# First layer of a two-layer scan network: the outer products of a pair of states split over two steps, a masking moved ahead of a product, parts of a softplus one step on

## The chip, the cores and the metric

The kernel runs on one core of a Trainium2 chip, in float32 throughout. The metric is the device time of one execution in microseconds. The core has five engines that each work through a list of their own and wait for each other by semaphores: TensorE (PE; PEld is its loading of weights), VectorE (DVE), ScalarE (ACT), GpSimd (POOL) and SyncE (SP), which here only starts DMA transfers. Matmul results go to PSUM, eight banks of 128 partitions with room for 512 float32 each; everything else is in SBUF or, between the stages, in DRAM.

## What is computed

Two layers of a vision state-space network, one behind the other, on 4 images of 64x64 positions and 192 channels. Each layer normalizes by groups, projects to 384 inner channels and a gate, scans the inner channels along the positions in four directions (by rows, by columns, and both backwards), normalizes the sum, multiplies by the gate and projects back. The change is in the first layer's scan. In the reference:

```python
delta = jax.nn.softplus(delta + delta_bias[None, :, None])
...
def step(h, inp):
    dt, ut, bt, ct = inp
    dA = jnp.exp(dt[..., None] * A_k[None])
    dBu = dt[..., None] * bt[:, :, None, :] * ut[..., None]
    h = dA * h + dBu
    y = jnp.einsum('bkdn,bkn->bkd', h, ct)
    return (h, y)
h0 = jnp.zeros((Bb, K, D, N), u.dtype)
...
_, ys = jax.lax.scan(step, h0, inps)
```

There are K = 4 directions, D = 384 channels, N = 16 states and 4096 positions. The matrix `A` is -n for state n = 1 to 16 (`A_logs` is the logarithm of 1 to 16 for every channel), so the decays of state n are the n-th powers of those of state 1.

## The kernel before

**Rounds and steps.** `FirstLayer.scans` does not walk position by position. It takes blocks of 30 positions (`RW`), the block of each of the four directions at once: 137 rounds (`NR`). Partitions 0 to 63 hold directions 0 and 1 (30 positions each, and four rows for the state carried over from the block before), partitions 64 to 127 directions 2 and 3; the free axis is 4 images x 384 channels = 1536 columns (`W`). A round has 16 steps, one for each state, from n = 16 down to n = 1 (`state(s) = NS - s % NS`); s counts steps through all rounds. So step 0 of a round has state 16, an even state belongs to an even step, and two states, an even step and the odd one behind it, make a pair.

**What one state needs.** Within a block the scan is a matrix product: the output at position l is the sum over the positions l' before it of C(l)·B(l') times the decay from l' to l times dt·u at l'. The decay is put into two factors.

- `outer(s)` (lines 1046 to 1055, TensorE) makes C(l)·B(l') for the two states of the pair (s, s+1) and all four images: two matmuls with a contraction of 8 rows, 128 columns of weights (`at_b`) and 256 columns of data (`cs`) each, into the two halves of one PSUM bank, tile `o`. The pool `pso` has one such tile, so a pair's first matmul waits until the pair before has been read.
- `cut_b(s)` (1057, VectorE) multiplies that bank, 128x512, by a mask that keeps l' up to l and writes `b` to SBUF. The pool has three of them.
- `grown(s)` (1062) makes `x`, dt·u times the n-th power of the growth at l'. For step 0 of a round it is a product of `dtu` with an exponential (line 1068); for each further step the tile of the step before times a factor `f` (line 1072). GpSimd does 1024 of the 1536 columns and VectorE 512, six steps ahead (`AHEAD`); seven tiles. In line 1068 VectorE's factor is the half bank `m[:, 1]` in PSUM (this is called the near product below), GpSimd's is `g` in SBUF.
- `mix(s, j)` (1074, TensorE) is the product itself, b times x, added into the accumulators. j is a half: a half is four 64x64 matmuls (two halves of the rows, two of the columns) with 384 columns of data, one in each quadrant of the array. `accs[0]` and `accs[1]`, two PSUM tiles of two banks, take half 0 and half 1.
- `weigh(s, j)` (1083, VectorE, line 1089) then multiplies accumulator j, 128x768, by the decay `fd`: with the states in falling order this is Horner's rule. In the last step `end_y` (line 962) does it and writes `y`.
- In every odd step ScalarE copies both accumulators to `sx` before they are weighed (`keep_end`, 1028), from which SyncE takes the rows of the carried state (`shrink`), ScalarE and GpSimd decay it (`decay`, `settle`) and SyncE writes it to DRAM (`carry_out`) for the next round (`carry_in`).

**What a round needs ahead of its first step.** `Round.steps` (974) lists this work with an offset in steps from the round's start and an engine; it runs among the steps of the rounds before, at the place `planned(s, engine)`. An offset of -20 is step 12 of a round, and -16 is step 0 of the round just ahead. A softplus of four products makes dt: `v(j)` (TensorE, one product for each half j), `parts(j)` (ScalarE: absolute value to `e`, relu to `up`), `exp(j)` (ScalarE, line 867: `e` becomes exp(-e)), `plus` (ScalarE, 871: `l` = e + 1), `rounded` (GpSimd, 875: `d` = l - 1), `log` (ScalarE, 878: `l` becomes its logarithm) and `delta(j, 0..3)` (TensorE: `up` + `e` - `d` + `l` summed up in PSUM tile `p` by products with a unit matrix). Then come `times_u`, `keep_dt`, sums along the block by a triangle matrix, and their exponentials. The products of this work that have a helper's shape all stand at line 845: eight 64x64 matmuls with 384 columns, or the 26-row form of `v`. Lines 899 and 913 are products of 128x128 with 512 columns. `sums_near` (913), `first_near` (916: the exponential into `m[:, 1]`), `fall_near` (920) and the near product follow each other in steps 9 and 10. The tile `p`, which is `m` in the code, exists once, so each of its uses waits for the readers of the use before. `steps` also lists `sums_d(0)` at -5, -3 and -2, whose results nobody reads.

**The order.** It is written out by hand (`tc.manual_schedule`): the loop over s at line 1094 issues the work of step s, and each engine gets its instructions in that order. TensorE's list of a step is: both halves of `mix(s + 1)`, the planned products, and in an even step `outer(s + 4)`. VectorE's is: both `weigh(s)`, `grown(s + 6)`, in an even step `cut_b(s + 2)`, the planned ones. ScalarE's is: in an odd step both copies, then the planned ones, then in an odd step `decay(s - 2)`. GpSimd's is: `grown(s + 6)`, in an odd step `settle(s - 4)`, the planned ones.

## Time and profile before

| | |
|---|---|
| three runs | 9029.12, 9060.8, 9049.5 us; median 9049.5 |
| the profiled execution | 9056.89 us, its span from first to last instruction 9055.1 |
| granted TensorE clock, mean over the span | 0.95 of full |
| VectorE's near products (L1068), first and last start | 695.5 and 7225.3 us, 137 of them |
| L1078, `mix` on TensorE | 35072 matmuls, mean 502 ns, 3552.2 us busy |
| L1089, `weigh` on VectorE | 4110, mean 958 ns, 195.2 us idle before them, 151.4 of it for TensorE's L1078 |
| L1028, copies on ScalarE | 2192, mean 800 ns, 1072.5 us idle before them, 1032.2 for TensorE's L1078 |
| L1072 on GpSimd | 2055, mean 2368 ns, 323.0 us idle before them |

One float32 matmul of the code is two matmul rows of the profile, so a step's product (both halves, four matmuls each) is a row with x16, the two outer products of a pair are x4 and a helper product is x8. Busy times of TensorE overlap: the end of a matmul is modelled, and the next one starts while it drains. Therefore the text below reads TensorE by the distance between the starts of its rows. In a timeline a bracket at the end of a row gives the engine's idle time just before it and the engine, tile and line that ended it. The stretches of the kernel ahead of the scan (the projections) and behind it (normalization, output, the whole second layer) are not touched.

### The profile page before, as it was taken

To read this page: it belongs to the slowest core of one execution; us is meant where nothing else is said; L and a number is where in the kernel's file an instruction comes from. 1 tells how busy PE (TensorE), PEld (TensorE's weight loads), DVE (VectorE), ACT (ScalarE), POOL (GpSimd) and SP (SyncE) were. 2 spreads that over 40 slices of the span, in tenths; PEclk is the share of its full clock that TensorE was granted. 3 is DMA by queue.
4 is the path that set the end of the run, shared out by engine and by line. 5 is a ranking of instruction groups with operands and counts; after the bars stand their busy time and mean duration, and the time that the engine had idled before them with its cause. 6 is when DMAs were issued, how large, how long until landed. Compare 5 with 4: busy or idle time off the path is not lost. (4 is left out here: it accounts for less than half of the span.)

```text
span 9055.1 us, 193788 instructions
## 1 busy us (share of the span) xinstructions
PE 8209.4 (91%) x64280; PEld 3630.8 (40%) x64280; DVE 7520.8 (83%) x10238; ACT 6193.2 (68%) x10104; POOL 6605.8 (73%) x3814
## 2 busy tenths in 40 slices
PE   8989999999999999999999999999999945786668
PEld 4433333333333333333333333333333335443457
DVE  3328999999999999989999999999999954786766
ACT  3337777777777777777777777777777745575668
POOL 0008999999999999999999999999999932001460
PEclk9999999999999999999999999999999977887789
DMA  6652333333332333333333333333333389343558
GB/s 186 212 183 65 74 76 75 79 74 75 76 78 73 75 78 77 74 77 83 82 84 86 83 83 83 82 83 83 82 83 83 83 211 252 107 138 125 162 140 284
DMA packets 952262, 971.20 MB, mean 107 GB/s; under 512 B 550175, under 2 KB 802732, under 8 KB 950368
## 3 DMA queue, kind: packets, MB, share of 16 engines
q1 hardware_dynamic: 946192, 951.97, 38.7%
q0 software_dynamic: 5056, 6.66, 0.6%
q8 instruction: 520, 8.52, 0.4%
q14 instruction: 494, 4.05, 0.1%
HBM read 521.83 MB, written 375.80 MB: 99 GB/s over the span
## 5 line engine op out<-in xcount | busy, mean ns | idle before, releaser
L1072 POOL TENSOR_TENSOR x<-x,f 128x1024 f32<-128x1024 f32 x2055 | 4865.9, 2368 | 323.0 <-issue 102.9
L1089 DVE TENSOR_TENSOR acc<-acc,fd 128x768 f32<-128x768 f32 x4110 | 3751.4, 958 | 195.2 <-PE acc L1078 151.4
L1078 PE MATMUL acc<-x,b 64*64 64x384 f32 x35072 | 3552.2, 502 | 69.2 <-DVE yt L962 62.6
L1028 ACT COPY sx<-acc 128x768 f32<-128x768 f32 x2192 | 1712.8, 800 | 1072.5 <-PE acc L1078 1032.2
L1078 PEld LDWEIGHTS acc<-x,b 64*64 64x64 f32 x35072 | 1056.2, 132 | 2084.6 <-DVE acc L1089 1397.3
L1072 DVE TENSOR_TENSOR x<-x,f 128x512 f32<-128x512 f32 x2055 | 1387.0, 675 | 0.1
L1052 PE MATMUL o<-cs,at_b 8*128 8x256 f32 x4384 | 1238.0, 401 | 3.7 <-DVE b L1060 3.5
L1052 PEld LDWEIGHTS o<-cs,at_b 8*128 8x128 f32 x4384 | 727.0, 184 | 772.4 <-DVE b L1060 363.1
L837 ACT ACTIVATE cs<-at_c,own 8x256 f32<-8x256 f32 x2192 | 979.8, 494 | 3.5 <-PE o L1052 3.5
L1060 DVE TENSOR_TENSOR b<-o,masks_f 128x512 f32<-128x512 f32 x1096 | 746.7, 681 | 5.7 <-PE o L1052 5.7
L462 PE MATMUL pp<-xT,w_in 96*128 96x512 f32 x1536 | 715.0, 617 | 20.9 <-ACT pad L1286 20.4
L875 POOL TENSOR_SCALAR d<-l 128x1536 f32<-128x1536 f32 x137 | 201.0, 1467 | 671.0 <-ACT l L871 669.9
L845 PE MATMUL p<-dt,steps_f 64*64 64x384 f32 x5480 | 580.0, 493 | 5.0 <-DVE dtu L890 1.9
L1300 DVE SCALAR_TENSOR_TENSOR acc<-pad,conv_w_s,acc 128x2048 f32<-128x2048 f32 x192 | 440.7, 2343 | 48.6 <-ACT acc L1298 47.4
L965 POOL TENSOR_TENSOR yt<-yt,yold 128x1536 f32<-128x1536 f32 x137 | 472.9, 3452 | 0.0
L929 ACT ACTIVATE fd<-p,shift 128x768 f32<-128x768 f32 x274 | 246.7, 900 | 300.2 <-PE p L845 300.2
L462 PEld LDWEIGHTS pp<-xT,w_in 96*128 96x128 f32 x1536 | 292.3, 197 | 370.3 <-issue 341.9
L1041 POOL TENSOR_TENSOR back<-back,small 128x96 f32<-128x96 f32 x1096 | 424.0, 387 | 14.4 <-DMA small<-sx 9.6
L549 PE MATMUL op<-w_out,v 128*128 128x192 f32 x1536 | 289.2, 346 | 136.8 <-DVE ot L552 92.4
L1038 ACT ACTIVATE back<-tot,late_f 128x96 f32<-128x96 f32 x1096 | 409.6, 374 | 0.0
L1281 POOL MEMSET pad<- 128x66 f32 x12 | 1.9, 159 | 553.6 <-DVE acc L1300 386.4
L1068 POOL TENSOR_TENSOR x<-dtu,g 128x1024 f32<-128x1024 f32 x137 | 324.4, 2368 | 80.2 <-ACT g L904 77.6
(218 smaller groups left out, 9542.8 us busy)
## 6 DMA issues: line engine op xcount, KB each, us to landing
x<-carry SPq DMA_DIRECT2D x4384, 24.0 KB
ut<-uT SPq DMA_DIRECT2D x548, 180.0 KB
small<-sx SPq DMA_DIRECT2D x2192, 24.0 KB
carry<-back SPq DMA_DIRECT2D x1096, 48.0 KB
zg<-gate SPq DMA_DIRECT2D x64, 768.0 KB
yold<-y_row SPq DMA_DIRECT2D x546, 90.0 KB
y_row<-yt SPq DMA_DIRECT2D x546, 90.0 KB
y_col<-yt SPq DMA_DIRECT2D x546, 90.0 KB
```

The costliest lines, as they stand in the source:

```text
L462: self.tc.nc.tensor.matmul(pp, self.w_in[:, i, e * 128 : (e + 1) * 128], self.xT[:, i, t * LC : (t + 1) * LC], start=(i == 0), stop=(i == ...
L837: nc.scalar.mul(self.cs[part][:, :, b, :], at_c[self.r % 2][:, at : at + PART, :], own[:, b : b + 1])
L845: nc.tensor.matmul(self.m[half(b), a, :DI], w(a, 2 * b + j), t(a, 2 * b + j), start=start and n == 0, stop=stop and n == len(terms) - 1, s ...
L965: nc.gpsimd.tensor_tensor(self.y, self.y, yold, ALU.add)
L1028: nc.scalar.copy(paired(sxs[s], j), accs[j][:, :, :DI])
L1041: nc.gpsimd.tensor_tensor(back[s], back[s], small[s], ALU.mult)
L1052: nc.tensor.matmul(outs[s][:, at], at_b[p][:, n, :], cs[:, n % PART].rearrange("q b l -> q (b l)"), start=True, stop=True, skip_group_chec ...
L1060: nc.vector.tensor_tensor(bs[s], o, bc(masks, 2, NB), ALU.mult)
L1072: engine.tensor_tensor(xs[s][:, part], xs[s - 1][:, part], f, ALU.mult)
L1078: nc.tensor.matmul(accs[j][half(c), r, :DI], bs[s - s % 2][half(r), s % 2, b, :], xs[s][half(r), cols(b)], start=s % NS == 0, stop=state(s ...
L1089: nc.vector.tensor_tensor(acc, acc, paired(of(s).fd, j), ALU.mult)
L1300: nc.vector.scalar_tensor_tensor(acc, part(tap), weight(tap), acc, ALU.mult, ALU.add)
```

## The change

Three things are changed, all in `FirstLayer.scans`.

1. `outer` takes the half h as an argument and issues one of the two matmuls. Half 0 stays where both were, at the end of an even step s, for the pair s + 4. Half 1 is issued in the next, odd step, between the two halves of that step's `mix`.
2. In the one step of a round in which `grown` on VectorE is the near product (step 10), `cut_b` now comes before it. In all other steps the order stays.
3. `exp(1)` goes from offset -18 to -17, `plus` from -17 to -16, `rounded` from -16 to -15 and `log` from -15 to -14. `exp(0)` and the products `delta` that read the results stay.

```diff
-                        r += [(2 * j - 20, "act", s(self.exp, j))]
+                        r += [(3 * j - 20, "act", s(self.exp, j))]
...
-                    r += [(-17, "act", self.plus), (-16, "pool", self.rounded), (-15, "act", self.log)]
+                    r += [(-16, "act", self.plus), (-15, "pool", self.rounded), (-14, "act", self.log)]
...
-            def outer(s):
-                outs[s] = ps_o.tile([128, LC], F32, name="o")
+            def outer(s, h):
+                if h == 0:
+                    outs[s] = ps_o.tile([128, LC], F32, name="o")
                 cs, p = of(s).cs[s % NS // PART], of(s).r % 2
-                for h in range(2):
-                    n = state(s) - 1 - h
-                    at = slice(h * NB * HALF, (h + 1) * NB * HALF)
-                    nc.tensor.matmul(
-                        outs[s][:, at], at_b[p][:, n, :], cs[:, n % PART].rearrange("q b l -> q (b l)"),
-                        start=True, stop=True, skip_group_check=True,
-                    )
+                n = state(s) - 1 - h
+                at = slice(h * NB * HALF, (h + 1) * NB * HALF)
+                nc.tensor.matmul(
+                    outs[s][:, at], at_b[p][:, n, :], cs[:, n % PART].rearrange("q b l -> q (b l)"),
+                    start=True, stop=True, skip_group_check=True,
+                )
...
-                    if on(s + AHEAD):
+                    if on(s + AHEAD) and (s + AHEAD) % NS > 0:
                         grown(s + AHEAD, nc.vector)
                     if on(s + 2) and s % 2 == 0:
                         cut_b(s + 2)
+                    if on(s + AHEAD) and (s + AHEAD) % NS == 0:
+                        grown(s + AHEAD, nc.vector)
                     planned(s, "dve")
-                    for j in range(2):
-                        if on(s + 1):
-                            mix(s + 1, j)
+                    if on(s + 1):
+                        mix(s + 1, 0)
+                    if on(s + 3) and s % 2 == 1:
+                        outer(s + 3, 1)
+                    if on(s + 1):
+                        mix(s + 1, 1)
                     planned(s, "pe")
                     if on(s + 4) and s % 2 == 0:
-                        outer(s + 4)
+                        outer(s + 4, 0)
```

## The prediction

> **What bounds the kernel now.** I read the page first, then one round of the first layer's scan through, engine by engine. The page says where the time is.

> ```profile
> PE 8209.4 (91%) x64280; PEld 3630.8 (40%) x64280; DVE 7520.8 (83%) x10238; ACT 6193.2 (68%) x10104; POOL 6605.8 (73%) x3814
> ...
> L1052 PE MATMUL o<-cs,at_b 8*128 8x256 f32 x4384 | 1238.0, 401 | 3.7 <-DVE b L1060 3.5
> ```

> The edit touches lines that run in the scan alone, 137 rounds of 16 steps: L1068 on VectorE, once a round, runs from 695.5 to 7225.3 us. The busy time of one round in the windows view (us; busy PE, PEld, DVE, ACT, POOL; clock):

> ```profile
> core 0: us, PE busy (x) PEld busy (x) DVE busy (x) ACT busy (x) POOL busy (x), PEclk, DMA share, GB/s
> 2500.22:2547.87 47.65, 46.15 (x422) 18.00 (x414) 44.55 (x60) 35.46 (x60) 45.20 (x27) 1.00 0.31 76
> ```

> 47.65 us a round. VectorE has 3.1 us to spare in it, GpSimd 2.5, TensorE by this row only 1.5, at the full granted clock. So TensorE comes first, and its rows have to be read by the distance between starts, since a matmul that is shown busy may overlap the next or hide a short wait. Its timeline (start, length, line, operands):

> ```profile
> 2500.58 1.12 PE L899 MATMUL p<-dt,steps_f 128*128 128x512 f32 x2
> 2501.64 1.13 PE L1052 MATMUL o<-cs,at_b 8*128 8x256 f32 x4
> 2502.69 1.52 PE L1078 MATMUL acc<-x,b 64*64 64x384 f32 x16
> 2504.03 0.82 PE L845 MATMUL p<-dt,steps_f 64*64 64x384 f32 x8
> ...
> 2509.89 1.13 PE L913 MATMUL p<-dt,steps_f 128*128 128x512 f32 x2
> 2510.95 1.52 PE L1078 MATMUL acc<-x,b 64*64 64x384 f32 x16
> 2513.24 0.88 PE L845 MATMUL p<-w_dtk_f,xd 26*64 26x384 f32 x8 [0.78 <-DVE x L1068]
> ...
> 2524.12 0.82 PE L845 MATMUL p<-dt,steps_f 64*64 64x384 f32 x8
> 2524.88 1.13 PE L1052 MATMUL o<-cs,at_b 8*128 8x256 f32 x4
> 2526.38 1.74 PE L1078 MATMUL acc<-x,b 64*64 64x384 f32 x16 [0.37 <-DVE yt L962]
> ...
> 2540.62 1.47 PE L1078 MATMUL acc<-x,b 64*64 64x384 f32 x16
> 2541.91 0.82 PE L845 MATMUL p<-d,minus_f 64*64 64x384 f32 x8
> 2542.56 0.82 PE L845 MATMUL p<-l,ident 64*64 64x384 f32 x8
> 2543.31 1.13 PE L1052 MATMUL o<-cs,at_b 8*128 8x256 f32 x4
> ```

> - A step's product with nothing to wait for: 2540.62 to 2541.91, 1.29, so 0.645 a half; a helper product of the same shape also 0.65 (2541.91 to 2542.56).
> - The block of outer products: 2501.64 to 2502.69, 1.055. A half product is two passes of 384 columns in 0.645, 0.84 ns a column; the block is four passes of 256, 0.86. The other 0.195 is its head and tail. L899 streams as many columns (2 x 512) and takes the same 1.06.
> - Entering it: a helper product followed by the block takes 0.75 (2542.56 to 2543.31), 0.11 more than 0.645. Leaving it: the product behind takes 1.34 (2502.69 to 2504.03), 0.05 more than 1.29.

> **What TensorE needs in a round.** 32 half products and 15 helper products at 0.645, three 512-column products and eight blocks at 1.055, 11 entries of 0.11 (six blocks, since two follow L899; three 512-column products; two of 26 rows), nine exits of 0.05: 30.3 + 3.2 + 8.4 + 1.2 + 0.45 = 43.6. The remaining 4.1 is waiting, more than the marked gaps show. 0.84 stands at 2513.24 (from 2510.95 it is 2.29, and the work 0.05 + 1.29 + 0.11 = 1.45), 0.45 at 2526.38 (the second half of the product before began 0.70 ahead of 2524.12, at 2523.42; 2.96 later the next can start, and 0.70 + 0.75 + 1.055 = 2.51 of work lies in that). 2.8 is small waits for VectorE's products with the decay.

> **The split of the outer products.** It takes nothing away and adds, eight times a round, a second head and tail (0.195), a second entry (0.11, now between two half products) and a second exit (0.05): 0.355 a pair, 2.84 a round. TensorE then needs 46.4. What it buys is that the product of an even step starts about 0.43 earlier, since only half a block (0.625) lies ahead of it; VectorE's 0.41 in front of the even steps' L1089 goes. But the second half of that product now stands behind the other half block: taking the round at 2501.64, its first half starts at 2502.26 in place of 2502.69, its second at 2502.26 + 0.70 + 0.11 + 0.625 = 2503.69 in place of 2503.39, 0.3 later, and VectorE waits there instead, at its second L1089. No new semaphore wait comes in: the half that moves reads rows of B and C that are loaded for the round, into a bank that the first half claimed. Queued behind it are the second half product, the planned products and the next half block; VectorE and ScalarE wait for the first.

> Which waits can take up the 2.84? Not the 0.84: L913, ScalarE's L916 and L920, VectorE's L1068 follow each other there, and no half block falls under them (the step's product is an odd one). The 0.45 grows: only 0.70 + 0.75 + 0.625 = 2.07 now lies in the 2.96, so 0.89. Of the small ones I can work out three kinds. Even steps behind one helper product: first half product to its end 0.82, copy 0.80, L1089 0.96, three handovers of 0.06, 2.75 in all, against 1.29 + 0.75 + 0.625 = 2.67 of work: 0.09, at three steps 0.27. The wait for the product with u (mark 0.35, by starts 0.53) loses 0.355 to the added work: 0.18. Behind the round's end, VectorE's chain over one pair is as long as TensorE's work, 4.0 each: 0 to 0.3. That is 0.6; further ones, where VectorE's 44.5 us of work don't fall into place, I can't add up by hand. Ends: 0.3 (nearly all covered) and 1.5 (half of the 2.8 kept). I take 0.9.

> Sum: 46.4 + 0.84 + 0.89 + 0.9 = 49.05, against 47.65: +1.4 a round, 137 rounds +192.

> The unknown in it is the price of a half block *inside* a product, which no row shows. Below, it could be nothing more than streaming (0 instead of 0.355), if loads and drains hide; above, 0.47, if the 0.11 is paid on leaving too. I take 0.355, since rows show every change of shape in both directions at one price.

> [...]

> **Masked B ahead of the near product.** VectorE's timeline:

> ```profile
> 2509.38 1.83 DVE L1089 TENSOR_TENSOR acc<-acc,fd 128x768 f32<-128x768 f32 x2 [0.41 <-PE acc L1078]
> 2512.50 0.69 DVE L1068 TENSOR_TENSOR x<-dtu,p 128x512 f32<-128x512 f32 x1 [1.29 <-issue]
> 2513.10 0.68 DVE L1060 TENSOR_TENSOR b<-o,masks_f 128x512 f32<-128x512 f32 x1
> ```

> L1060 (0.60 from start to start) moves into the 1.29 of idle time; L1068 stays at 2512.50, because it waits for ScalarE's L920, which ends at 2512.41. VectorE is 0.6 earlier behind it, but its next L1089 waits for a ScalarE copy that ends at 2513.14, and the step after for TensorE, whose next product goes through L1068, the helper product and the block. I take 0, ends -0.5 and 0 a round. Were the idle time gone, it would delay L1068 by 0.6.

> **The second exponential, plus, rounding and logarithm one step on.** No instruction is added. ScalarE's queue: L867 (0.73) goes behind two copies that started at 2523.50 after 0.37 idle, so it delayed nothing and now can't; L871 then starts near 2526.9 and ends near 2528.4. GpSimd's L875 falls behind one product of 2.33 and one of 0.35: 2531.45 in place of 2528.77, and TensorE reads it at 2533.42. L878 follows, done by about 2533.7, read at 2535.60; ScalarE's next copies started at 2534.99. 1.9 us of slack each: 0. What covers it is the idle 1.96 and 1.23 in front of ScalarE's copies; without it L878's 1.4 would come on top.

> All is a difference to the profiled execution (9056.89, span 9055.1), 0.08% above the median of 9049.5, so it is added to the median: 9242.

> **Rivals.**
> - *The half block costs only its streaming.* With a price e a pair the round is 43.6 + 8e + 0.84 + 0.89 + 0.9 = 46.2 + 8e. It decides at e = 0.18: below that the kernel is faster; at 0, 46.2, -1.44 x 137 = -197: 8852. For it: 2.8 us of small waits lie in just the places where the half now goes. Against it: the 0.11, 0.195 and 0.05 at every change of shape in the rows. 7%.
> - *The waits swallow the price.* e between 0.16 and 0.20: 9022 to 9077, within 0.3%, about what a measurement of this kernel can tell from no change. Against it: two of the larger waits stay or grow. 5%.
> - *All of it on the path.* 2.84 x 137 = +389: 9438; or the sum above with L878 late by 1.4, 9434. For it: TensorE's 91%. Against it: the waits for VectorE that later products no longer see. 7%.
> - The forecast, a sum with small waits of 0.3 to 1.5 and e of 0.28 to 0.40: 9077 to 9376, 81%.

> Faster 7%, same 5%, slower 88%. The range 9110 to 9365 leaves out the two outer rivals and the forecast's lowest edge.

> **What would show it.** L1052's mean goes from 401 to some 428 ns (its median is 374, so the first of four, with its load in view, takes 482; now it is the first of two); its rows stand alone with 0.62 to the next product, and inside a step's product in every odd step; L1068 on VectorE repeats every 49 us; the idle time of L1089 for TensorE grows from 151 us to over 400; L875 and L878 gain no waiters. A half block under 0.5 us, or a round under 47.65, would prove me wrong; L845's helper products waiting for L875 or L878 would put the loss in the wrong place.

## The result, and the profile after

The changed kernel takes 9492.6 us (median of 4 runs, 9491.47 to 9501.06) against 9052.73 for the one before (9029.12 to 9060.8): a ratio of 1.0492, 95% interval 1.0472 to 1.0513. It is 440 us slower. The forecast was 192 slower, and the time lies above its range.

The page after, with the lines that answer to those shown of before, and the granted clock in 40 slices of the span:

```profile
PE 8627.3 (91%) x64280; PEld 3630.6 (38%) x64280; DVE 7635.2 (80%) x10238; ACT 6174.1 (65%) x10104; POOL 6608.2 (70%) x3814
...
PEclk9989999999999999999999999999999986888688
...
L1089 DVE TENSOR_TENSOR acc<-acc,fd 128x768 f32<-128x768 f32 x4110 | 3843.0, 961 | 580.8 <-PE acc L1078 331.5
...
L1052 PE MATMUL o<-cs,at_b 8*128 8x256 f32 x4384 | 1549.0, 433 | 1.6 <-DVE b L1060 1.2
```

All of it is in the scan: from the first near product to the last it takes 6970.2 us, 6529.8 before, 440 more. The distances between near products tell more than their mean. Before, 101 of the 136 lie within 0.1 of 47.65 us. After, they come in two kinds: 34 are 49.0, and most of the others are 50.5 or 52.2. The windows view of three rounds of the changed kernel in a row (us; busy PE, PEld, DVE, ACT, POOL; granted clock; DMA share and GB/s):

```profile
2122.11:2174.33 52.22, 50.58 (x414) 18.66 (x414) 45.39 (x60) 35.23 (x60) 45.51 (x27) 0.93 0.29 72
2174.33:2226.58 52.25, 50.53 (x414) 18.35 (x414) 45.48 (x59) 35.36 (x60) 44.94 (x27) 0.93 0.29 71
2226.58:2275.58 49.00, 47.28 (x414) 17.39 (x414) 45.34 (x59) 35.25 (x60) 45.16 (x27) 1.00 0.29 72
```

The short round has the full clock, the long ones 0.93 of it. The instructions are the same. Here is TensorE at the start of the short round, with the end of the round behind it:

```profile
2227.32 0.87 PE L845 MATMUL p<-w_dtk_f,xd 26*64 26x384 f32 x8 [0.77 <-DVE x L1068]
2228.12 0.69 PE L1052 MATMUL o<-cs,at_b 8*128 8x256 f32 x2
2228.75 0.88 PE L1078 MATMUL acc<-x,b 64*64 64x384 f32 x8
2229.55 0.69 PE L1052 MATMUL o<-cs,at_b 8*128 8x256 f32 x2
2230.18 0.88 PE L1078 MATMUL acc<-x,b 64*64 64x384 f32 x8
2230.88 0.82 PE L845 MATMUL p<-dt,steps_f 64*64 64x384 f32 x8
...
2239.22 0.69 PE L1052 MATMUL o<-cs,at_b 8*128 8x256 f32 x2
2240.75 0.88 PE L1078 MATMUL acc<-x,b 64*64 64x384 f32 x8 [0.83 <-DVE yt L962]
```

A half block costs 0.63 to the next product (2228.12 to 2228.75), the half product in front of the inner half block 0.80 (0.645 + 0.05 for leaving a half block + 0.11 for entering the next), the half product behind it 0.70. That is the forecast's price, row by row. The wait at the round's end is 1.53 - 0.63 = 0.90. And VectorE waits where it was to wait, at its second L1089 of an even step:

```profile
2231.12 0.97 DVE L1089 TENSOR_TENSOR acc<-acc,fd 128x768 f32<-128x768 f32 x1 [0.47 <-PE acc L1078]
```

Now the same place in the long round before it. A half product takes 1.10 and 1.34 in place of 0.80 and 0.70, a helper product 1.28 in place of 0.64, and from 2183.95 on the products take what they take in the short round:

```profile
2175.07 0.87 PE L845 MATMUL p<-w_dtk_f,xd 26*64 26x384 f32 x8 [0.78 <-DVE x L1068]
2175.87 0.69 PE L1052 MATMUL o<-cs,at_b 8*128 8x256 f32 x2
2176.50 1.17 PE L1078 MATMUL acc<-x,b 64*64 64x384 f32 x8
2177.60 1.21 PE L1052 MATMUL o<-cs,at_b 8*128 8x256 f32 x2
2178.74 1.56 PE L1078 MATMUL acc<-x,b 64*64 64x384 f32 x8
2180.08 1.50 PE L845 MATMUL p<-dt,steps_f 64*64 64x384 f32 x8
2181.36 2.66 PE L1078 MATMUL acc<-x,b 64*64 64x384 f32 x16
2183.95 0.88 PE L845 MATMUL p<-w_dtk_f,xd 26*64 26x384 f32 x8
```

The trace's records of the granted clock, each a stretch with one value, say what that is: 0.5 of full from 2176.95 to 2183.78, two steps of 3.413 us. The windows view of this stretch and of the one behind it:

```profile
2176.95:2183.78 6.83, 6.83 (x42) 2.28 (x34) 3.60 (x6) 3.27 (x6) 2.95 (x3) 0.50 0.41 101
2183.78:2190.61 6.83, 6.83 (x66) 2.62 (x62) 5.56 (x8) 5.09 (x10) 5.12 (x4) 1.00 0.31 72
```

All half-clock records of the scan start on one grid of 3.413 us and last whole steps of it. Such a step is called a window below, and the place of an instruction within it the phase. In the scan there are 25 before (92 us in sum) and 138 after (645 us), 86 of these behind the near product's wait and 52 behind the one at the round's end.

So the 440 us are 136 x (49.00 - 47.65) = 184 at full clock, and 257 that the half clock adds: the mean round of 51.25 lies 2.25 above the full-clock round, that of before, 48.01, 0.36 above its own.

Why so many more? Before, over a long stretch the half clock came every tenth round, at 1462.41, 1940.28, 2418.14 and 2896.01: 47.65 us are 13.96 windows. From round to round the long wait slides by 0.04 of a window over the grid, until it meets a bad phase, one at which half clock follows. That costs 1.4 us, which pushes it 0.4 of a window away, for ten rounds. After, 49.00 us are 14.36 windows and a long round of 52.25 is 15.31: from round to round the wait moves by about a third of a window and is soon back in the bad phase. The expectations call this the clock theory; it, its parts and its rivals are what the runs were for.

### The profile page after: what moved, and what is told of

It reads as the page before. It is cut to its first block, busy times and chain, and to the rows that moved or that the text cites. A ratio compares the mean times of both kernels' runs of the same rounds, so it can differ in the third digit from the quotient of the medians.

```text
span 9491.1 us, 193381 instructions
## 1 busy us (share of the span) xinstructions
PE 8627.3 (91%) x64280; PEld 3630.6 (38%) x64280; DVE 7635.2 (80%) x10238; ACT 6174.1 (65%) x10104; POOL 6608.2 (70%) x3814
## 5 line engine op out<-in xcount | busy, mean ns | idle before, releaser
L1089 DVE TENSOR_TENSOR acc<-acc,fd 128x768 f32<-128x768 f32 x4110 | 3843.0, 961 | 580.8 <-PE acc L1078 331.5
L1078 PE MATMUL acc<-x,b 64*64 64x384 f32 x35072 | 3778.1, 524 | 131.4 <-DVE yt L962 117.0
L1028 ACT COPY sx<-acc 128x768 f32<-128x768 f32 x2192 | 1644.2, 800 | 994.2 <-PE acc L1078 943.5
L1078 PEld LDWEIGHTS acc<-x,b 64*64 64x64 f32 x35072 | 1100.0, 138 | 1916.2 <-DVE acc L1089 754.5
L1052 PE MATMUL o<-cs,at_b 8*128 8x256 f32 x4384 | 1549.0, 433 | 1.6 <-DVE b L1060 1.2
L837 ACT ACTIVATE cs<-at_c,own 8x256 f32<-8x256 f32 x2192 | 985.7, 496 | 514.0 <-PE o L1052 514.0
L1052 PEld LDWEIGHTS o<-cs,at_b 8*128 8x128 f32 x4384 | 651.6, 185 | 1370.3 <-issue 862.0
L1060 DVE TENSOR_TENSOR b<-o,masks_f 128x512 f32<-128x512 f32 x1096 | 748.6, 683 | 5.7 <-PE o L1052 5.7
L875 POOL TENSOR_SCALAR d<-l 128x1536 f32<-128x1536 f32 x137 | 201.2, 1469 | 667.3 <-ACT l L871 667.3
L845 PE MATMUL p<-dt,steps_f 64*64 64x384 f32 x5480 | 627.6, 530 | 5.0 <-DVE dtu L890 1.9
L845 PE MATMUL p<-w_dtk_f,xd 26*64 26x384 f32 x2192 | 244.0, 513 | 125.5 <-DVE x L1068 106.8
```

Source lines behind the costliest of these rows:

```text
L837: nc.scalar.mul(self.cs[part][:, :, b, :], at_c[self.r % 2][:, at : at + PART, :], own[:, b : b + 1])
L845: nc.tensor.matmul(self.m[half(b), a, :DI], w(a, 2 * b + j), t(a, 2 * b + j), start=start and n == 0, stop=stop and n == len(terms) - 1, s ...
L1028: nc.scalar.copy(paired(sxs[s], j), accs[j][:, :, :DI])
L1052: nc.tensor.matmul(outs[s][:, at], at_b[p][:, n, :], cs[:, n % PART].rearrange("q b l -> q (b l)"), start=True, stop=True, skip_group_chec ...
L1060: nc.vector.tensor_tensor(bs[s], o, bc(masks, 2, NB), ALU.mult)
L1078: nc.tensor.matmul(accs[j][half(c), r, :DI], bs[s - s % 2][half(r), s % 2, b, :], xs[s][half(r), cols(b)], start=s % NS == 0, stop=state(s ...
```

## The experiments

The table is worked out from the traces: the median distance of near products over rounds without a half-clock record, the mean over all, and the half-clock records (in all; behind the near product; behind the round's end).

```
kernel                  time us   round, full clock   mean    half clock
before                  9052.73   47.65               48.01    25   19   6
after                   9492.60   49.00               51.25   138   86  52
e1 split alone          9505.12   48.92               51.33   142   85  57
e2 no split             9041.41   47.65               47.92    17   15   2
e3 warm                 9189.87   49.06               49.15     2    1   1
e4 padded               9368.63   49.14               50.36   100   99   1
e5 warm end             9353.00   49.07               50.27    64   63   1
e6 outer in near wait   8976.27   47.11               47.41     9    0   9
e7 fill, no idle        8970.80   47.11               47.46    18    0  18
e8 eight rows           9275.36   49.06               49.66    38   37   1
```

**e1 and e2: which part of the change.** e1 has the split alone, e2 the other two parts alone, as in the diff above.

> Only the split of the outer products; masking and softplus stay where they were. Clock theory: the split makes both parts of the loss, TensorE's work (rounds of 49.0 us at full clock, 137 x 1.34 = +184 us) and half-clock windows behind the round's two long waits: 9400 to 9520 us, with more than 90 half-clock records in the scan. Rival, that the moved masking or the later softplus make the rounds of 52.2 us: about 9235 us, nearly no half-clock windows.

> Masking ahead of the near product and softplus one step on, outer products as before. Clock theory: nothing on TensorE's path changes, 9030 to 9075 us, rounds of 47.65. Rival, that these two parts cost the 255 us that the sum did not have: about 9300 us.

e1: 9505.12, ratio 1.0499 (1.0480 to 1.0518). e2: 9041.41, ratio 0.9987 (0.9974 to 0.9999). The split makes the whole loss. The other two parts leave the round at 47.65; the little that e2 gains goes with eight half-clock windows fewer. Beside the split they cost 0.08 us a round at full clock (49.00 against 48.92); which of the two does was not tried.

**e3: keep the array working in the two waits.** The changed kernel with

```diff
-                    r += [(at, "pe", s(self.sums_d, 0)) for at in (-5, -3, -2)]
+                    r += [(at, "pe", s(self.sums_d, 0)) for at in (-5, -3, -2, -2)]
...
+                    if on(s + AHEAD) and (s + AHEAD) % NS == 0:
+                        outs[s + 4] = ps_o.tile([128, LC], F32, name="o")
+                        nc.tensor.matmul(
+                            outs[s + 4][:, :DI], tri, of(s + AHEAD).dt[:, :DI],
+                            start=True, stop=True, skip_group_check=True,
+                        )
                     planned(s, "pe")
```

Where this added product stands, `outer` doesn't claim the tile `o` a second time.

> The changed kernel with two extra TensorE products a round whose results are overwritten or not read: a 128x128 product of 384 columns into the free bank of the outer products, in the wait for the near product, and one more 64x64 helper product (8 matmuls) in front of the wait at the round's end. They keep the array working in these two waits. Clock theory: rounds of 49.0 to 49.2 us, nearly no half-clock windows: 9180 to 9260 us, 230 to 310 faster than the changed kernel though TensorE does more. Rival, that the rounds of 52.2 us come from late results and the half clock only goes with them: 9490 us or more.

9189.87 us, ratio 1.0142 (1.0123 to 1.0161): 303 us faster than the changed kernel, with 1.4 us more of work on TensorE in each round. A round of it in the windows view (columns as above):

```profile
2100.00:2149.06 49.06, 48.86 (x428) 17.89 (x424) 45.35 (x60) 35.25 (x61) 45.16 (x27) 1.00 0.30 74
```

PE is busy for 48.86 of 49.06 us and the clock stays full. This separates the two parts of the loss: with nearly no half clock (2 records) the split costs 137 us, which is about the forecast's 1.4 us a round (192) less the 49 us of half clock that the kernel before had. Half-clock windows are the cause of the long rounds, not their companion.

**e4: the same length without the split.** The kernel before with two more unread helper products in places where they lengthen the round.

```diff
-                    r += [(at, "pe", s(self.sums_d, 0)) for at in (-5, -3, -2)]
+                    r += [(at, "pe", s(self.sums_d, 0)) for at in (-5, -5, -3, -3, -2)]
```

> The kernel before with two more helper products a round (in steps 11 and 13, results not read), no split: some 1.4 us of full-activity work, the round as long as the changed kernel's at full clock, 49.0 to 49.2. Clock theory: the old round of 47.65 us was 13.96 windows of 3.413 us, so the long wait met the bad phase only once in ten rounds; at 49.1 it meets it at every third or so: 9270 to 9400 us, more than 40 half-clock records in the scan. Rival, that the split itself makes the low activity: 137 x 1.45 = +199, 9250 us with no more half-clock windows than before (25).

9368.63, ratio 1.0343 (1.0324 to 1.0361), 100 half-clock windows, 99 of them behind the near product. The block of outer products is whole here, and the added products have nearly all of the array's cells at work (in before eight rows of 64x64 weights and 384 columns go through in 0.645 us; by the weighting used at e8 their cells work 8 x 0.25 x 0.32 = 0.64 us); still the windows are four times as many as before. So the kernel before was spared by the length of its round. The phases at which the near products of the two traces start show it: of those in the first 0.3 of a window, half clock followed within 8 us in 8 of 8 before and in 71 of 71 in e4, and of those between 0.4 and 0.9 in 1 of 94 and in none of 22. The bad phases are the same; e4's rounds fall on them far more often. The 52 behind the round's end, of which e4 has one, do come from the split: it leaves a longer wait there (0.90 for 0.45), with a half block (8 of 128 rows of weights) ahead of it and another, one half product later, behind it.

**e5: only the round's end kept at work.** The changed kernel with the first edit of e3.

> The changed kernel with only the second extra product of e3: one more helper product (0.64 us) in front of the wait at the round's end. Clock theory: that wait is 0.89 us, so the rounds at full clock stay at 49.0 to 49.1; the half-clock windows behind the round's end (52 in the changed kernel) go, those behind the near product (86) stay in part, since the phase of each round is another: 9270 to 9400 us. Rival, that one of the two places alone makes all the loss: 9190 or 9490.

9353.00, ratio 1.0331 (1.0314 to 1.0348). The windows behind the round's end go from 52 to 1, those behind the near product from 86 to 63. So the round's end alone gives 140 of e3's 303 us; the near product's wait alone was not tried.

**e6 and e7: use the wait.** If masked B is ready before the near product, its bank is free, and the next block of outer products can run in the wait for the near product instead of behind it. No split; part 2 of the change, and

```diff
+                    near = (s + AHEAD) % NS == 0
+                    if on(s + 4) and near:
+                        outer(s + 4)
                     planned(s, "pe")
-                    if on(s + 4) and s % 2 == 0:
+                    if on(s + 4) and s % 2 == 0 and not near:
                         outer(s + 4)
```

e7 also drops the three unread products and puts the first of the softplus sum in the place of one.

```diff
-                    r += [(at, "pe", s(self.delta, 0, i)) for i, at in enumerate((-17, -16, -15, -14))]
+                    r += [(at, "pe", s(self.delta, 0, i)) for i, at in enumerate((-18, -16, -15, -14))]
...
-                    r += [(at, "pe", s(self.sums_d, 0)) for at in (-5, -3, -2)]
+                    r += [(at, "pe", s(self.sums_d, 0)) for at in ()]
```

> No split. Masked B ahead of the near product, and in that one step of the round the whole block of outer products (1.055 us) ahead of the planned helper product, so in TensorE's wait of 0.84 for the near product instead of behind it. Critical-path theory: VectorE's near product releases the helper product and the next step's product with no block between them; the round at full clock falls by 0.4 to 0.5 to about 47.2, and the wait no longer joins the block to one long stretch of low activity, so the half-clock windows (25) nearly go: 9050 - 60 - 45, 8930 to 8970 us. Rival, that another wait (VectorE for the copies) takes its place: 9000 to 9050 us.

> e6 without the three helper products whose results nobody reads, and the first product of the softplus sum one step earlier, in the place of the third. 1.9 us less of TensorE work a round. Chain theory: this work lay beside the chain of VectorE's and TensorE's turns, so the round at full clock stays at 47.2 and the time within 0.5% of e6, unless half-clock windows return. Rival, that TensorE's throughput is the bound: up to 137 x 1.9 = 260 us less, 8690 us.

e6: 8976.27, ratio 0.9922 (0.9908 to 0.9936). e7: 8970.80, ratio 0.9911 (0.9895 to 0.9926). Both beat both kernels; e6's round came out as expected, its time 6 us above the expected range. TensorE in e7:

```profile
2530.00 1.52 PE L1078 MATMUL acc<-x,b 64*64 64x384 f32 x16
2531.45 1.13 PE L1052 MATMUL o<-cs,at_b 8*128 8x256 f32 x4
2532.50 0.87 PE L845 MATMUL p<-w_dtk_f,xd 26*64 26x384 f32 x8
2533.31 1.67 PE L1078 MATMUL acc<-x,b 64*64 64x384 f32 x16
2535.57 1.74 PE L1078 MATMUL acc<-x,b 64*64 64x384 f32 x16 [0.59 <-DVE acc L1089]
```

The block stands between the product and the helper product, with no mark of a wait; the next product follows 0.81 behind the helper's start. Neither has a half-clock window behind the near product. And e7 does 1.9 us less of work than e6 in a round of the same 47.11 us; TensorE waits that much more, as at 2535.57. So those three products lay beside what binds in e6. That this is the chain of turns between VectorE's L1089 and TensorE's L1078, with what stands between the two products of an odd and an even step, is my reading; no run tested it alone. The room isn't wide: e4's two more such products lengthened the round of the kernel before by 1.49 us.

**e8: what does the clock count?** e3 with an 8-row product in place of the 128-row one (against the changed kernel, beside e3's first edit):

```diff
+                    if s > 0 and on(s + AHEAD) and (s + AHEAD) % NS == 0:
+                        outer(s + 4, 0)
                     planned(s, "pe")
                     if on(s + 4) and s % 2 == 0:
                         outer(s + 4, 0)
```

> As e3, but the product that fills the wait for the near product has 8 rows of weights in place of 128: the first half block of outer products is issued there too, 0.62 us, and overwritten by its second issue. TensorE is busy in the wait either way. If the clock follows the share of the array's cells that work in a window, the 8-row product hardly counts: half-clock windows behind the near product as in e5 (63), 9330 to 9370 us. Rival, that it follows the time in which any matmul runs: they go as in e3 (2), 9180 to 9230 us.

9275.36, ratio 1.0248 (1.0229 to 1.0268): between the two; neither number was right. The count of half-clock windows also hangs on which phases the rounds fall on, so it is a bad witness. The windows themselves are a better one. For every window of the grid in the scans of all ten traces with the full clock, I worked out two shares: the time in which some matmul streams, and the same with each matmul weighted by its rows x columns of weights over 128 x 128 cells, the largest weights of any row (0.83 ns a column streamed, ahead of the last 0.16 us of its row: an estimate from the rows of before, most of which take 0.374 us for 256 columns and 0.482 for 384). Each share is set against the clock of the next window.

```
                        18,728 windows, 549 of them followed by half clock
share of cells at work  best limit 0.36: 27 on the wrong side
share of time busy      best limit 0.58: 338 on the wrong side
in e8, followed by half clock: cells up to 0.350, time up to 0.725
in e8, followed by full clock: cells from 0.361, time from 0.680
```

In e8 windows that were busy for up to 0.725 of their time were followed by the half clock, and others, busy from 0.680 on, were not; by cells the two don't overlap (up to 0.350, from 0.361). The limits are those that fit these windows best; no run was made to test them on new ones.

## Why the prediction was wrong in size

**Right, and shown.** The price of a half block inside a product, the one number that no row had, is about 0.355 a pair as taken: the rows above have each of its three terms. The waits that can't be filled: the one before the near product's successor kept its mark (0.78 before, 0.77 after), the one at the round's end has 0.90 for 0.89. VectorE's wait moved to its second L1089. The round at full clock is 49.00 for 49.05. That it is so close is in part luck: the sum's last term, 0.9 of small waits, was chosen between 0.3 and 1.5, and no run shows it but as the rest. e2 shows that the masking and the later softplus cost nothing by themselves, as taken, though L875 did gain a waiter: L878 waits for it (27.7 us in 85 rounds, 1.6 in one before). TensorE's products wait for L878 in one round, as they did before.

**The step that failed** is the first one: "at the full granted clock". The forecast read one round with a clock of 1.00, took every duration from it, and multiplied by 137. It priced work and waits and never the clock that the waits set; its rivals share that. The missing term is the 257 us. The profile of before had it in view, though small: a clock of 0.99 over the scan (the 0.95 of the span comes mostly from the 0.80 behind the scan), 25 half-clock records in it, and 18 rounds of 49.0 to 49.1 us among those of 47.65, each with a record behind the near product. The sum used neither the spread of the rounds nor the records. With them it could have had a term for a wait that grows from 0.45 to 0.89 between two half blocks that use 8 of 128 rows, and one for a round that no longer fits the grid.

**A wait that was denied.** "No new semaphore wait comes in" holds for TensorE's half block, but not for what reads behind it: ScalarE's L837, which writes `cs`, now waits 514.0 us for the later L1052 (3.5 before). In the full-clock round shown this is 3.4 us on ScalarE, and VectorE's marked waits for ScalarE there are 0.67 and 0.20 us, as they were before (0.64 and 0.20), so little of it can be in the 1.35 us.

**Half right.** TensorE's work was taken as the bound and the sum made of what it needs plus what it must wait. The number came out, but e7 shows that TensorE could do 1.9 us less in e6's order without a shorter round. My reading, which no run shows for the split, is that the number holds because the split puts its price on the chain of turns. "All of it on the path" (9438) came nearest to the time, for a reason that has nothing to do with it.

**Signs named.** L1052's mean is 433 for 428, the half clock included. L1089's idle time for TensorE went from 151 to 331.5 us, not over 400; that for ScalarE's copies grew too, from 40.9 to 194.9, and all of it from 195.2 to 580.8.

## What to carry to other kernels

Before you multiply one round by their number, see how the rounds differ and which clock was granted in the long ones: a stretch of low TensorE activity was paid twice here, as a wait (0.78 us at 2175.07) and as slow matmuls behind it (1.10 and 1.34 us for half products that take 0.80 and 0.70 at full clock). Splitting a block of matmuls to fill a wait bought a second change of shape on both sides here, 0.355 us a pair by the rows; see whether the whole block fits into a wait elsewhere (here, after a masking that frees its bank), which gave 0.8% in e6. Set the length of a round against the steps of the clock's records too: here the round of 47.65 us, 13.96 steps of 3.413, had 25 half-clock records in the scan, and the same kernel with two more helper products, 49.14 in e4 (14.40 steps), had 100.
